# Gram matrix in two 64-column halves of the array, with a quarter of the redistribution copied by ScalarE

## The chip, the core and the metric

The kernel runs on one core of a Trainium2 chip. The metric is the device time of one execution in microseconds (us), the median of three runs. Everything is computed in 32-bit floats.

## The reference

Two identical bottleneck layers follow each other on a tensor of 64 images, 1024 channels and 14 x 14 pixels (12,544 pixels over all images). Biases, scales and shifts are inputs, and every normalisation takes its mean and variance over all images and pixels:

```python
def _conv(x, w, b, stride, pad):
    y = jax.lax.conv_general_dilated(x, w, window_strides=(stride, stride), padding=[(pad, pad), (pad, pad)], ...)
    return y + b.reshape(1, -1, 1, 1)
def _bn(x, gamma, beta):
    mean = jnp.mean(x, axis=(0, 2, 3), keepdims=True)
    var = jnp.var(x, axis=(0, 2, 3), keepdims=True)
    xn = (x - mean) * jax.lax.rsqrt(var + EPS)
    return gamma.reshape(1, -1, 1, 1) * xn + beta.reshape(1, -1, 1, 1)
# one layer; x has 1024 channels, the middle has 256
out = jax.nn.relu(_bn(_conv(x, w1, b1, 1, 0), g1, be1))      # 1x1, 1024 -> 256
out = jax.nn.relu(_bn(_conv(out, w2, b2, 1, 1), g2, be2))    # 3x3, 256 -> 256
out = _bn(_conv(out, w3, b3, 1, 0), g3, be3)                 # 1x1, 256 -> 1024
out = jax.nn.softplus(residual_scale)[0] * out
return jax.nn.relu(x + out)
```

## The kernel before

The 256 middle channels of all 12,544 pixels stay in SBUF as one tile `y_all`: 128 partitions, two channel slots `s`, 12,544 pixels. Each layer has the stages conv1 (1x1), conv2 (3x3, by a fast algorithm with few products), then a stage called the Gram stage here, then conv3 (1x1) with the residual.

The Gram stage exists because the third normalisation needs the mean and the variance of conv3's output before that output is used. Instead of computing conv3 twice, the kernel computes the 256 x 256 Gram matrix of the normalised conv2 output over all pixels (the sum over pixels of channel times channel) and the channel sums. From these and the weights `conv3_stats` (L1099) gets the mean and variance of all 1024 output channels.

For a Gram matrix the array needs pixels on the partitions, while `y_all` has channels there. So `gram` (L994) makes transposed tiles `zt`: 128 pixels on the partitions, two such blocks per tile (`CH = 2`), and 256 channels plus a column of ones along the row. There are six `zt` buffers. 12,544 pixels are 98 blocks, taken two at a time: 49 pairs.

- Normalising: `norm_to` (L1012) goes through `y_all` in pieces. ScalarE applies scale, shift and relu (L544), then VectorE subtracts a constant per channel (`less`, L1010), once for each of the two slots. The pieces have 256, 512, 1536, 832 and then six times 1568 pixels; the six are called A to F here.
- The first seven pairs (`FIRST = 7`) go by TensorE: four 128 x 128 transposes into PSUM (L1040), then one VectorE copy into `zt` (L1046).
- The other 42 pairs go by VectorE's 32 x 32 block transpose (`by_vector`, L1049). That needs the four 32-channel groups brought onto the right partitions first. `spread(k)` (L1024) does so for 1536 pixels at a time, `k = 0 .. 6`, six pairs each: sixteen transfers, from partition group `j` to partition group `i` for all `i, j`, each of 32 partitions x 2 slots x 384 pixels (96 KB). Nine are issued on SP's queue and seven on POOL's. In the four with `i == j` the data keep their partitions. The target `homes[k % 2]` is one of two buffers, so `spread(k + 2)` can only begin when the transposes of `spread(k)` have read it. The buffers are named `ws` and `home` in the first layer, `home` both in the second.
- The products: for each block of 128 pixels two matmuls, `cp` with 128 channels as the stationary operand and 257 columns moving (channels 0 to 255 and the ones), and `ap` with the other 128 channels and 129 columns. The part below the diagonal is not computed. In the trace every 32-bit matmul appears as two passes, each with a weight load of its own (x2 in the rows).

```python
matmul(g0, before[:, c, 0:P], before[:, c, :], start=first, stop=last)
matmul(g1, before[:, c, P:M], before[:, c, P:], start=first, stop=last)
```

`conv3_stats` scales the two PSUM results into SBUF (`g0` on VectorE, L1106, `g1` on ScalarE, L1107), doubles the part above the diagonal (`off`, L1108), multiplies by the weights in two halves of 512 columns with three matmuls each (L1123 to L1125), multiplies elementwise by the weights (L1128) and adds over partitions with a ones operand. A matmul group of conv3 that is needed later anyway stands in TensorE's queue between the last Gram matmul and the first of `conv3_stats`.

Order: matmuls, and instructions wrapped in `tc.keep_in_program_order` (`less`, the copies, the transposes, everything through `act`), stand in their engine's queue as written. Others are placed by a scheduler. `pairs` (L1059) is the generator that sets the order by hand: its table `then` says after which of the first seven pairs a piece is normalised or a `spread` is issued.[...]

Of the kernel before, what the change touches and what calls it, by code (L numbers as in the profile page):

```python
# [37 lines left out]
FP = mybir.dt.float32  # L38
AF = mybir.ActivationFunctionType
ALU = mybir.AluOpType  # L40

P = 128
N, C, H, W = 64, 1024, 14, 14
HW = H * W
M = 256
CS = C // P
MS = M // P
# [5 lines left out]
NPX = N * HW  # L53
CH = 2
NZT = 6

FIRST, LAST = 7, 0
RUN = 3 * P
STEP = 4 * RUN
# [7 lines left out]
GPX = GI * HW  # L67
# [20 lines left out]
def bottlenecks(ctx: ExitStack, tc: tile.TileContext, x, w1s, w2s, w3s, pars, out):  # L88
    nc = tc.nc
# [5 lines left out]
    y_all = keep.tile([P, MS, NPX], FP, tag="y", name="y")  # L95
# [70 lines left out]
    def matmul(*args, **kw):  # L166

        tc.keep_in_program_order(nc.tensor.matmul(*args, **kw))  # L168
# [160 lines left out]
    def act(*args, **kw):  # L329

        tc.keep_in_program_order(nc.scalar.activation(*args, **kw))  # L331
# [209 lines left out]
    def norm(s, y, aff, act=nc.scalar.activation):  # L541

        scale, shift = aff
        act(y, y, AF.Relu, bias=shift[:, s : s + 1], scale=scale[:, s : s + 1])  # L544
# [449 lines left out]
    def gram(psum, pool, homes, aff, minus_c, beside):  # L994

        g0, g1 = psum.tile(M + 1, "cp"), psum.tile(P + 1, "ap")
        zts = [pool.tile([P, CH, M + 1], FP, tag=f"zt{i}", name=f"zt{i}") for i in range(NZT)]
        for zt in zts:  # L1000
            nc.gpsimd.memset(zt[:, :, M:], 1.0)
        zts = itertools.cycle(zts)

        head = 3 * CH * P
        start = FIRST * CH * P
        bounds = [0, CH * P, head, head + STEP, *range(2 * GPX, NPX + 1, GPX)]
        pieces = list(zip(bounds, bounds[1:]))

        def less(s, y):
            tc.keep_in_program_order(nc.vector.tensor_scalar(y, y, minus_c[:, s : s + 1], None, ALU.add))  # L1010

        def norm_to(end):  # L1012

            while pieces and pieces[0][0] < end:
                a, e = pieces.pop(0)
                for s in reversed(range(MS)):
                    y = y_all[:, s, a:e]
                    if a == 0 and s == 1:
                        norm_vector(s, y, aff, minus_c[:, s : s + 1])
                    else:  # L1020
                        norm(s, y, aff)
                        less(s, y)

        def spread(k):  # L1024

            first = start + k * STEP if k else head
            norm_to(first + STEP)
            x = homes[k % 2][:, : MS * STEP].rearrange("p (s j f) -> p s j f", s=MS, j=4)
            for i, j in itertools.product(range(4), range(4)):
                queue = nc.gpsimd if 4 * i + j in (1, 3, 6, 8, 10, 13, 15) else nc.sync  # L1030
                a = first + i * RUN
                queue.dma_start(out=x[32 * i : 32 * i + 32, :, j], in_=y_all[32 * j : 32 * j + 32, :, a : a + RUN])
            return x.rearrange("p s j f -> p (s j) f")

        def by_tensor(a):
            tp = psum.tile(CH * M)
            for c in range(CH):
                for s in range(MS):
                    tc.keep_in_program_order(
                        nc.tensor.transpose(  # L1040
                            tp[:, (c * MS + s) * P : (c * MS + s + 1) * P],
                            y_all[:, s, a + c * P : a + (c + 1) * P], ident,
                        )
                    )
            zt = next(zts)
            tc.keep_in_program_order(nc.vector.tensor_copy(zt[:, :, :M], tp.rearrange("p (c m) -> p c m", c=CH)))  # L1046
            return zt

        def by_vector(x, i):  # L1049
            zt = next(zts)  # L1050
            tc.keep_in_program_order(
                nc.vector.transpose(
                    zt[:, :, :M].rearrange("p b (n c) -> p b n c", c=32),
                    x[:, :, i * CH * 32 : (i + 1) * CH * 32].rearrange("p n (b r) -> p b n r", r=32),
                )
            )
            return zt

        def pairs():  # L1059

            norm_to(head)
            then = {
                1: lambda: ready.append(spread(0)),
                2: partial(norm_to, 2 * GPX),
                4: partial(norm_to, 3 * GPX),
                5: lambda: ready.append(spread(1)),
            }
            for i in range(FIRST):
                a = i * CH * P
                yield by_tensor(a if a < head else a + STEP)  # L1070
                if i == 0:
                    busy(psum, "ax", 1)
                if i in then:
                    then[i]()
            for k in range(STEPS):
                x = ready.pop(0)
                for i in range(RUN // (CH * 32)):
                    yield by_vector(x, i)
                if k + 2 < STEPS:
                    ready.append(spread(k + 2))  # L1080
            norm_to(NPX)
            for i in range(LAST):
                yield by_tensor(NPX - (LAST - i) * CH * P)

        ready = []
        total = NPX // (CH * P)
        before = None
        for k, zt in enumerate(itertools.chain(pairs(), (None,))):
            if before is not None:
                for c in range(CH):  # L1090
                    first, last = k == 1 and c == 0, k == total and c == CH - 1
                    matmul(g0, before[:, c, 0:P], before[:, c, :], start=first, stop=last)
                    matmul(g1, before[:, c, P:M], before[:, c, P:], start=first, stop=last)
            before = zt
            if k in beside:
                beside[k]()
        return g0, g1

    def conv3_stats(psum, one, grams, w3, mv, tags, spare):  # L1099


        g0p, g1p = grams
        g0 = one.tile([P, M + 1], FP, tag="g0", name="g0")
        g1 = one.tile([P, P + 1], FP, tag="g1", name="g1")
        off = one.tile([P, P], FP, tag="goff", name="goff")
        nc.vector.tensor_scalar(g0, g0p, 1.0 / NPX, None, ALU.mult)  # L1106
        nc.scalar.activation(g1, g1p, AF.Copy, scale=1.0 / NPX)  # L1107
        nc.vector.tensor_scalar(off, g0[:, P:M], 2.0, None, ALU.mult)  # L1108
        means = g0[:, M:], g1[:, P:]
        wide = 64  # L1110
        sums = [psum.tile(CS * wide, tag).rearrange("p (o k) -> p o k", k=wide) for tag in ("ax", "ap")]
        ones = one.tile([P, 1], FP, tag="ones", name="ones")
        nc.vector.memset(ones, 1.0)
        ones = ones[:, :1].to_broadcast([P, wide])
        by_mean, w = spare[:, :C], [w3[:, s].rearrange("p o c -> p (o c)") for s in range(MS)]
        nc.vector.tensor_scalar(by_mean, w[0], means[0], None, ALU.mult)
        nc.vector.scalar_tensor_tensor(by_mean, w[1], means[1], by_mean, ALU.mult, ALU.add)
        half = CS // 2
        q = one.tile([P, MS, C], FP, tag="q", name="q")
        for h in range(2):  # L1120
            cols = slice(h * half, (h + 1) * half)
            t0, t1 = (psum.tile(half * P, tag) for tag in tags[2 * h : 2 * h + 2])
            matmul(t0, g0[:, 0:P], w3[:, 0, cols, :], start=True, stop=True)  # L1123
            matmul(t1, off, w3[:, 0, cols, :], start=True, stop=False)
            matmul(t1, g1[:, 0:P], w3[:, 1, cols, :], start=False, stop=True)  # L1125
            qs = [q[:, s, h * half * P : (h + 1) * half * P] for s in range(MS)]
            for s, t in ((0, t0), (1, t1)):
                nc.vector.tensor_mul(qs[s], t, w3[:, s, cols, :].rearrange("p o c -> p (o c)"))  # L1128
            nc.vector.tensor_add(qs[0], qs[0], qs[1])
        for o in range(CS):  # L1130
            matmul(sums[0][:, o], by_mean[:, o * P : (o + 1) * P], ones, start=True, stop=True)
        for o in range(CS):
            matmul(sums[1][:, o], q[:, 0, o * P : (o + 1) * P], ones, start=True, stop=True)
        nc.vector.tensor_copy(mv[:, :, 0], sums[0][:, :, 0])
        nc.vector.tensor_copy(mv[:, :, 1], sums[1][:, :, 0])
        sq = small.tile([P, CS], FP, tag="sq", name="sq")
        nc.vector.tensor_mul(sq, mv[:, :, 0], mv[:, :, 0])
        nc.vector.tensor_sub(mv[:, :, 1], mv[:, :, 1], sq)
# [193 lines left out]
    with tc.tile_pool(name="first", bufs=1) as one, tc.tile_pool(  # L1332
        name="first_x", bufs=4
# [133 lines left out]
```

## Time and profile before

| | us |
|---|---|
| median of 3 runs | 1944.43 |
| lowest and highest | 1944.18, 1944.73 |
| the profiled execution's own time | 1944.06 |
| its span in the trace | 1942.3 |
| Gram stage of layer 0: first ScalarE normalisation | 586.49 |
| first matmul of pair 7 | 602.63 |
| first matmul after the last Gram product | 659.77 |
| the same three in layer 1 | 1552.01, 1568.15, 1624.75 |

The last rows are start times within the span. From the first normalisation to the end of the Gram products it takes 73.3 us in layer 0 and 72.7 us in layer 1. "Idle before" at the end of a row is the time in which the engine had nothing to do before that row's first instruction, with what ended it. Times given as "offset" in what follows count from the first ScalarE normalisation of the layer.

### The profile page before, as it was taken

The numbers are of one execution on the slowest core, as the hardware profiler recorded it, in microseconds if no ns is written. First come the engines' busy times: TensorE is split into PE (matmuls) and PEld (weight loads), VectorE is DVE, ScalarE is ACT, GpSimd is POOL, SyncE is SP. The second block draws the span as 40 slices with busy tenths as digits, with TensorE's granted clock in tenths as the row PEclk, the third lists the DMA queues.
The fourth block names the chain that finished last, engine by engine and source line by source line (L and its number), as shares of the span: only waits on it lengthen the run. The fifth ranks groups of instructions, "written<-read, shape, count | busy, mean of one in ns | idle before, by whom it ended". The sixth has DMA issues, their size and how long they took to land.

```text
span 1942.3 us, 27081 instructions
## 1 busy us (share of the span) xinstructions
PE 1918.6 (99%) x9438; PEld 1612.1 (83%) x9438; DVE 1544.3 (80%) x2473; ACT 1046.2 (54%) x2098; POOL 575.1 (30%) x674
## 2 busy tenths in 40 slices
PE   9999999999999999999999999999999999999999
PEld 5555557999997799999999999989999987555555
DVE  5778667999998667776776767689999975888886
ACT  2222214677765055555555555456777651666666
POOL 0111100212105133433333334302121051666664
PEclk9999999999999999999999999999999999999999
DMA  7777634887948634444444444258788486899998
GB/s 291 273 250 263 235 129 157 204 221 202 230 141 207 197 137 187 175 166 166 181 185 167 166 178 180 108 181 209 215 208 225 140 194 233 279 334 335 333 342 300
DMA packets 201849, 413.91 MB, mean 213 GB/s; under 512 B 37809, under 2 KB 178001, under 8 KB 185201
## 3 DMA queue, kind: packets, MB, share of 16 engines
q1 hardware_dynamic: 161728, 324.66, 49.0%
q0 software_dynamic: 34368, 36.45, 9.3%
q10 hardware_dynamic: 5616, 51.06, 6.3%
q8 instruction: 75, 1.23, 0.3%
q14 instruction: 62, 0.50, 0.1%
HBM read 263.75 MB, written 115.34 MB: 195 GB/s over the span
## 4 chain that ended last, share of the span: by engine, by line
PE 92%; DVE 5%; DMA 1%; ACT 1%; issue 1%; SPq 0%; POOL 0%; DVEq 0%; ACTq 0%
PE cy L168 17%; PE ay L168 17%; PE columns L168 13%; PE cp L168 12%; PE ap L168 10%; PE m L168 6%; PE l L168 6%; PE cx L168 5%; PE ax L168 4%; PE ps L168 1%; DMA home<-y 1%; ACT y L544 1%; DVE v L628 0%; DVE sums L622 0%; DVE steps L697 0%
## 5 line engine op out<-in xcount | busy, mean ns | idle before, releaser
L331 ACT ACTIVATE cu<-cy,scale 128x196 f32<-128x196 f32 (+1 forms) x552 | 256.7, 474 | 277.5 <-PE cy L168 271.3
L168 PE MATMUL columns<-v,ub 128*128 128x224 f32 (+1 forms) x1536 | 300.7, 337 | 0.0
L331 ACT ACTIVATE x<-x,shift 128x392 f32<-128x392 f32 x428 | 241.1, 613 | 59.5 <-POOL x L490 53.1
L168 PEld LDWEIGHTS columns<-v,ub 128*128 128x128 f32 x1536 | 269.2, 188 | 2.8
L464 DVE SCALAR_TENSOR_TENSOR x<-cp,scale,x 128x196 f32<-128x196 f32 (+1 forms) x368 | 178.2, 484 | 97.2 <-PE cp L168 96.1
L168 PE MATMUL cy<-ct,ws 128*128 128x196 f32 (+1 forms) x736 | 221.9, 383 | 1.1 <-ACT cu L331 1.1
L485 POOL TENSOR_TENSOR x<-x,cu 128x196 f32<-128x196 f32 (+1 forms) x184 | 159.3, 866 | 172.1 <-ACT cu L331 162.5
L168 PE MATMUL ay<-at,ws 128*128 128x196 f32 (+1 forms) x752 | 209.1, 381 | 0.0
L490 POOL TENSOR_TENSOR x<-x,cu 128x392 f32<-128x392 f32 x124 | 125.9, 1016 | 192.8 <-DVE x L464 188.1
L168 PEld LDWEIGHTS ay<-at,ws 128*128 128x128 f32 x752 | 136.5, 190 | 33.4
L168 PEld LDWEIGHTS cy<-ct,ws 128*128 128x128 f32 x736 | 133.3, 190 | 36.4 <-ACT cu L331 4.2
L168 PE MATMUL l<-diffs,ub 128*128 128x224 f32 (+1 forms) x768 | 149.1, 337 | 2.6 <-PE columns L168 2.6
L511 POOL TENSOR_TENSOR x<-x,cu 128x392 f32<-128x392 f32 x120 | 121.9, 1017 | 85.9 <-DVE x L464 62.4
L168 PE MATMUL m<-sums,ua 128*128 128x224 f32 (+1 forms) x752 | 145.9, 337 | 1.5 <-DVE sums L622 1.5
L168 PEld LDWEIGHTS l<-diffs,ub 128*128 128x128 f32 x768 | 134.3, 189 | 4.4 <-PE columns L168 3.9
L331 ACT ACTIVATE au<-ay 128x196 f32<-128x196 f32 (+1 forms) x141 | 53.8, 381 | 155.2 <-PE ay L168 152.4
L464 DVE SCALAR_TENSOR_TENSOR x<-cx,scale,x 128x196 f32<-128x196 f32 (+1 forms) x184 | 89.1, 484 | 57.4 <-PE cx L168 57.4
L168 PEld LDWEIGHTS m<-sums,ua 128*128 128x128 f32 x752 | 131.3, 189 | 3.3 <-DVE sums L622 2.9
L168 PE MATMUL cx<-y,w 128*128 128x196 f32 (+1 forms) x404 | 124.1, 392 | 0.4 <-DVE x L1148 0.4
L168 PE MATMUL cy<-y,w 128*128 128x196 f32 (+1 forms) x404 | 123.8, 392 | 0.0
L168 PE MATMUL cp<-zt 128*128 128x257 f32 x392 | 118.0, 382 | 1.8 <-DVE zt L1046 1.7
L168 PE MATMUL cp<-y,ws 128*128 128x196 f32 (+1 forms) x368 | 113.6, 390 | 0.9 <-DVE x L464 0.9
(216 smaller groups left out, 3924.8 us busy)
## 6 DMA issues: line engine op xcount, KB each, us to landing
x<-in_x SPq DMA_DIRECT2D x62, 1568.0 KB, 6.8
ub<-u SPq DMA_DIRECT2D x94, 768.0 KB, 5.2
x<-mid SPq DMA_DIRECT2D x32, 1568.0 KB, 8.2
mid<-x ACTq DMA_DIRECT2D x31, 1568.0 KB, 5.1
out<-x SPq DMA_DIRECT2D x123, 392.0 KB, 5.7
ua<-u SPq DMA_DIRECT2D x94, 256.0 KB, 3.0
u<-y POOLq DMA_DIRECT2D x48, 256.0 KB, 5.8
home<-y SPq DMA_DIRECT2D x90, 96.0 KB, 4.3
```

Source lines behind the costliest of these rows:

```text
L168: tc.keep_in_program_order(nc.tensor.matmul(*args, **kw))
L331: tc.keep_in_program_order(nc.scalar.activation(*args, **kw))
L464: nc.vector.scalar_tensor_tensor(v, bank, self.scale[:, o : o + 1], v, ALU.mult, ALU.add)
L485: nc.gpsimd.tensor_add(self.part(1, 1), self.part(1, 1), u3)
L490: nc.gpsimd.tensor_add(v, v, self.u12)
L511: nc.gpsimd.tensor_add(v, v, self.u12[:, i * self.n : (i + 1) * self.n])
L544: act(y, y, AF.Relu, bias=shift[:, s : s + 1], scale=scale[:, s : s + 1])
```

## The change

There are three parts.

1. The products. The 256 channels are taken as four quarters of 64. For each block of 128 pixels there are now four matmuls with 64 stationary columns each, two in the left half of the array's columns and two in the right half (`tile_position`), with 193, 193, 129 and 130 moving columns. `zt` has a column of ones at both ends (258 wide). Each quarter is multiplied with the quarters after it, and the corner (quarter 3 with quarter 0) is taken in the last one, whose moving operand is in two pieces.
2. The statistics. The four PSUM pieces are scaled into two tiles by multiplication with constant tiles `by` (1 or 2 over the number of pixels), and the weight products take four matmuls per half instead of three.
3. The redistribution. `spread` issues only the twelve transfers with `i != j`, seven on SP and five on POOL. The new `stay(k)` makes the other four copies on ScalarE, in program order, and the normalisations go through `act` too, so that their place among the copies is fixed: `stay(0)` stands after the 832-pixel piece and ahead of A, `stay(1)` ahead of C, `stay(2)` ahead of E, `stay(3)` ahead of F, and `stay(4)` to `stay(6)` after all of them. On VectorE the `less` of D moves up, so that C and D both stand between the transposes of `spread(0)` and those of `spread(1)`.

```diff
+Q = P // 2
...
-        g0, g1 = psum.tile(M + 1, "cp"), psum.tile(P + 1, "ap")
-        zts = [pool.tile([P, CH, M + 1], FP, tag=f"zt{i}", name=f"zt{i}") for i in range(NZT)]
+        upper, lower = psum.tile(3 * Q + 1, "cp"), psum.tile(2 * Q + 2, "ap")
+        zts = [pool.tile([P, CH, M + 2], FP, tag=f"zt{i}", name=f"zt{i}") for i in range(NZT)]
         for zt in zts:
-            nc.gpsimd.memset(zt[:, :, M:], 1.0)
+            nc.gpsimd.memset(zt[:, :, 0 : M + 2 : M + 1], 1.0)
...
+        def ends(v):
+            (step, n), (_, _) = v.ap
+            return bass.AP(v.tensor, v.offset + 1, [[step, n], [3 * Q, 2], [1, Q + 1]])
...
+        by = [pool.tile([P, n], FP, tag=f"by{i}", name=f"by{i}") for i, n in enumerate((3 * Q + 1, 2 * Q + 2))]
+        gs = [pool.tile([P, M + 2], FP, tag=f"g{i}", name=f"g{i}") for i in range(MS)]
...
-                        norm(s, y, aff)
+                        norm(s, y, aff, act)
                         less(s, y)
+        def home(k):
+            return homes[k % 2][:, : MS * STEP].rearrange("p (s j f) -> p s j f", s=MS, j=4)
+        def first_of(k):
+            return start + k * STEP if k else head
+        def stay(k):
+            for i in range(4):
+                here, a = slice(32 * i, 32 * i + 32), first_of(k) + i * RUN
+                act(home(k)[here, :, i], y_all[here, :, a : a + RUN], AF.Copy)
         def spread(k):
-            first = start + k * STEP if k else head
+            first = first_of(k)
             norm_to(first + STEP)
-            x = homes[k % 2][:, : MS * STEP].rearrange("p (s j f) -> p s j f", s=MS, j=4)
-            for i, j in itertools.product(range(4), range(4)):
-                queue = nc.gpsimd if 4 * i + j in (1, 3, 6, 8, 10, 13, 15) else nc.sync
+            x = home(k)
+            for n, (i, j) in enumerate(itertools.permutations(range(4), 2)):
+                queue = nc.gpsimd if n in (1, 3, 6, 8, 10) else nc.sync
...
                 1: lambda: ready.append(spread(0)),
-                2: partial(norm_to, 2 * GPX),
+                2: lambda: (norm_to(2 * GPX), stay(0)),
                 4: partial(norm_to, 3 * GPX),
-                5: lambda: ready.append(spread(1)),
+                5: lambda: (ready.append(spread(1)), stay(1)),
...
                 if k + 2 < STEPS:
                     ready.append(spread(k + 2))
+                    norm_to(first_of(k + 2) + 2 * STEP)
+                    stay(k + 2)
...
-                    matmul(g0, before[:, c, 0:P], before[:, c, :], start=first, stop=last)
-                    matmul(g1, before[:, c, P:M], before[:, c, P:], start=first, stop=last)
+                    v = before[:, c]
+                    for q, with_ in enumerate((v[:, : 3 * Q + 1], v[:, Q + 1 :], v[:, 2 * Q + 1 :], ends(v))):
+                        here = slice(q % 2 * Q, q % 2 * Q + Q)
+                        to = (upper, lower)[q // 2][here]
+                        to = to[:, : 2 * Q + 1] if q == 2 else to
+                        if q == 3:
+                            to = to.rearrange("p (k m) -> p k m", k=2)
+                        matmul(
+                            to, v[:, 1 + q * Q : 1 + q * Q + Q], with_, start=first, stop=last,
+                            tile_position=(0, q % 2 * Q), skip_group_check=True,
+                        )
...
-        nc.vector.tensor_scalar(g0, g0p, 1.0 / NPX, None, ALU.mult)
-        nc.scalar.activation(g1, g1p, AF.Copy, scale=1.0 / NPX)
-        nc.vector.tensor_scalar(off, g0[:, P:M], 2.0, None, ALU.mult)
+        def scaled(g, a, ps, by):
+            nc.vector.tensor_mul(g[:, a : a + ps.shape[1]], ps, by[:, : ps.shape[1]])
+        scaled(g0[low], 0, upper[low], by[0][low])
+        scaled(g0[high], Q + 1, upper[high], by[0][high])
+        scaled(g1[low], 2 * Q + 1, lower[low, : 2 * Q + 1], by[1][low])
+        n = Q + 1
+        for a, k in (1, 0), (3 * Q + 1, 1):
+            scaled(g1[high], a, lower[high, k * n : k * n + n], by[1][high, k * n : k * n + n])
+        nc.scalar.activation(g0[high, 0:1], g0[high, M + 1 :], AF.Copy)
...
-            matmul(t0, g0[:, 0:P], w3[:, 0, cols, :], start=True, stop=True)
-            matmul(t1, off, w3[:, 0, cols, :], start=True, stop=False)
-            matmul(t1, g1[:, 0:P], w3[:, 1, cols, :], start=False, stop=True)
+            for i, g in enumerate((g0, g1)):
+                for n, t in enumerate((t0, t1)):
+                    matmul(t, g[:, 1 + n * P : 1 + n * P + P], w3[:, i, cols, :], start=i == 0, stop=i == 1)
```

More of the change, by code (lines that the diff above doesn't have):

```diff
@@ L994, in gram @@
     def gram(psum, pool, homes, aff, minus_c, beside):
-        g0, g1 = psum.tile(M + 1, "cp"), psum.tile(P + 1, "ap")
-        zts = [pool.tile([P, CH, M + 1], FP, tag=f"zt{i}", name=f"zt{i}") for i in range(NZT)]
+        upper, lower = psum.tile(3 * Q + 1, "cp"), psum.tile(2 * Q + 2, "ap")
+        zts = [pool.tile([P, CH, M + 2], FP, tag=f"zt{i}", name=f"zt{i}") for i in range(NZT)]
         for zt in zts:
-            nc.gpsimd.memset(zt[:, :, M:], 1.0)
+            nc.gpsimd.memset(zt[:, :, 0 : M + 2 : M + 1], 1.0)
         zts = itertools.cycle(zts)
+        def ends(v):
[3 more added lines that the diff above has]
+        gs = [pool.tile([P, M + 2], FP, tag=f"g{i}", name=f"g{i}") for i in range(MS)]
+        once, twice = 1.0 / NPX, 2.0 / NPX
+        for g in gs:
+            nc.gpsimd.memset(g, 0.0)
+        low, high = slice(0, Q), slice(Q, P)
+        for i, here, cols, value in (
+            (0, low, slice(0, Q + 1), once), (0, low, slice(Q + 1, 3 * Q + 1), twice),
+            (0, high, slice(0, Q), once), (0, high, slice(Q, 3 * Q), twice),
+            (0, high, slice(3 * Q, 3 * Q + 1), once),
+            (1, low, slice(0, Q), once), (1, low, slice(Q, 2 * Q), twice), (1, low, slice(2 * Q, 2 * Q + 1), once),
+            (1, high, slice(0, Q), twice), (1, high, slice(Q, Q + 1), 0.0), (1, high, slice(Q + 1, 2 * Q + 2), once),
+        ):
+            nc.gpsimd.memset(by[i][here, cols], value)
         head = 3 * CH * P
@@ L1045, in by_tensor @@
             zt = next(zts)
-            tc.keep_in_program_order(nc.vector.tensor_copy(zt[:, :, :M], tp.rearrange("p (c m) -> p c m", c=CH)))
+            tc.keep_in_program_order(
+                nc.vector.tensor_copy(zt[:, :, 1 : M + 1], tp.rearrange("p (c m) -> p c m", c=CH))
+            )
             return zt
@@ L1052, in by_vector @@
                 nc.vector.transpose(
-                    zt[:, :, :M].rearrange("p b (n c) -> p b n c", c=32),
+                    zt[:, :, 1 : M + 1].rearrange("p b (n c) -> p b n c", c=32),
                     x[:, :, i * CH * 32 : (i + 1) * CH * 32].rearrange("p n (b r) -> p b n r", r=32),
@@ L1091, in gram @@
                     first, last = k == 1 and c == 0, k == total and c == CH - 1
-                    matmul(g0, before[:, c, 0:P], before[:, c, :], start=first, stop=last)
-                    matmul(g1, before[:, c, P:M], before[:, c, P:], start=first, stop=last)
+                    v = before[:, c]
[8 more added lines that the diff above has]
+                            tile_position=(0, q % 2 * Q), skip_group_check=True,
+                        )
             before = zt
@@ L1096, in gram @@
                 beside[k]()
-        return g0, g1
+        return upper, lower, by, gs
     def conv3_stats(psum, one, grams, w3, mv, tags, spare):
[L1102 to L1105, printed above, removed]
-        nc.vector.tensor_scalar(g0, g0p, 1.0 / NPX, None, ALU.mult)
-        nc.scalar.activation(g1, g1p, AF.Copy, scale=1.0 / NPX)
-        nc.vector.tensor_scalar(off, g0[:, P:M], 2.0, None, ALU.mult)
-        means = g0[:, M:], g1[:, P:]
+        upper, lower, by, (g0, g1) = grams
+        low, high = slice(0, Q), slice(Q, P)
+        def scaled(g, a, ps, by):
[7 more added lines that the diff above has]
+        nc.scalar.activation(g0[high, 0:1], g0[high, M + 1 :], AF.Copy)
+        means = g0[:, 0:1], g1[:, M + 1 :]
         wide = 64
```

## The prediction

> **What bounds the kernel now.** I read the page first (its busy times, then the costliest groups), then the busy times by stretch of the Gram stage, then the timelines of TensorE, VectorE and ScalarE there.
>
> ```profile
> PE 1918.6 (99%) x9438; PEld 1612.1 (83%) x9438; DVE 1544.3 (80%) x2473; ACT 1046.2 (54%) x2098; POOL 575.1 (30%) x674
> ...
> L168 PE MATMUL cp<-zt 128*128 128x257 f32 x392 | 118.0, 382 | 1.8 <-DVE zt L1046 1.7
> ```
>
> TensorE is busy 99% of the span, so a stage is worth what its matmuls cost. The busy time by stretch, for the start, the steady part and the statistics of layer 0, and the first two of layer 1:
>
> ```profile
> 586.50:602.60 16.10, 13.39 (x81) 10.75 (x79) 13.45 (x22) 16.10 (x13) 7.00 (x10) 1.00 0.83 225
> 602.60:659.80 57.20, 57.09 (x345) 52.06 (x346) 39.20 (x60) 10.00 (x7) 23.15 (x40) 1.00 0.92 245
> 659.80:669.75 9.95, 9.95 (x50) 6.52 (x49) 6.85 (x12) 0.28 (x1) 0.00 (x0) 1.00 0.11 21
> 1552.00:1568.10 16.10, 13.40 (x81) 10.75 (x79) 13.44 (x22) 16.09 (x13) 6.98 (x10) 1.00 0.64 165
> 1568.10:1624.80 56.70, 56.65 (x345) 51.94 (x346) 36.72 (x55) 10.02 (x7) 23.06 (x40) 1.00 0.94 265
> ```
>
> Columns: stretch, length, busy TensorE, weight loads, VectorE, ScalarE, POOL, granted clock, share of the DMA engines, GB/s. At the start ScalarE is full and TensorE is not. From 602.6 on TensorE is full, and so, nearly (0.92), are the DMA engines. TensorE's timeline:
>
> ```profile
> 602.63 0.70 PE L168 MATMUL cp<-zt 128*128 128x257 f32 x2 [0.85 <-DVE zt L1046]
> 603.16 0.39 PE L168 MATMUL ap<-zt 128*128 128x129 f32 x2
> 603.39 0.60 PE L168 MATMUL cp<-zt 128*128 128x257 f32 x2
> 603.82 0.38 PE L168 MATMUL ap<-zt 128*128 128x129 f32 x2
> 604.04 0.60 PE L168 MATMUL cp<-zt 128*128 128x257 f32 x2
> ...
> 661.09 1.02 PE L168 MATMUL cy<-w,g 128*128 128x512 f32 x2
> 661.94 1.02 PE L168 MATMUL cp<-w,goff 128*128 128x512 f32 x2
> 662.80 1.02 PE L168 MATMUL cp<-w,g 128*128 128x512 f32 x2
> 663.66 1.02 PE L168 MATMUL cy<-w,g 128*128 128x512 f32 x2
> ```
>
> Start to start is what counts: a block takes 0.655 us (603.39 to 604.04), a 512-column matmul 0.86 us (661.09 to 661.94). A line through 512 columns (860 ns) and 386 columns in two matmuls (655 ns) gives 2 passes x (0.833 ns a column + about 3 ns). 43 pairs from pair 7 to the end are 86 x 0.655 = 56.4 us of the 57.14 between 602.63 and 659.77.
>
> The engines that feed it:
>
> ```profile
> 586.49 26.11 ACT L544 ACTIVATE y<-y,shift,scale 128x256 f32<-128x256 f32 x19 [1.08 <-DVE shift L1277]
> ...
> 597.51 1.98 DVE L1010 TENSOR_SCALAR y<-y,minus_c 128x1568 f32<-128x1568 f32 x2
> 600.00 1.98 DVE L1010 TENSOR_SCALAR y<-y,minus_c 128x1568 f32<-128x1568 f32 x2
> 601.88 0.69 DVE L1046 COPY zt<-ay 128x512 f32<-128x512 f32 x1
> 602.53 3.68 DVE L1052 STREAM_TRANSPOSE zt<-ws 128x512 f32<-128x512 f32 x6
> 606.13 1.94 DVE L1010 TENSOR_SCALAR y<-y,minus_c 128x1568 f32<-128x1568 f32 x2
> 611.24 3.68 DVE L1052 STREAM_TRANSPOSE zt<-home 128x512 f32<-128x512 f32 x6 [3.17 <-DMA home<-y]
> ...
> 606.24 6.48 SPq L1032 DMA_DIRECT2D ws<-y  x9
> ```
>
> ScalarE normalises without a break for 26.1 us. VectorE's queue mixes `less` with the transposes; whatever `less` waits for, the transposes behind it wait for. The transfers of one `spread` take about 10 us from first issue to last landing, and from the second spread's transposes (611.24) to the seventh's (647.33 in the same timeline) is 36.1 us, 7.2 us per spread, beside TensorE's 6 x 1.31 = 7.9.
>
> **Part 1, the products.** 64 stationary columns: passes of 193 columns take 161 + 3 = 164 ns, of 129 or 130 columns 111. Nothing in this trace shows two matmuls in two halves of the array, so the block is bounded from both sides. If both halves run freely beside each other, a half has 2 x (164 + 111) = 550 ns a block, against 655. If the halves run one after the other, 1100 ns. Weight loads: sixteen 64-column matmuls (`ax<-ones,home`, from 666.24 to the next group at 667.97) come every 108 ns, though 64 moving columns need 56, so a 128-column load takes 108 ns. If 64 columns load in half of that, eight loads take 432 ns and lie beside the 550; if not, 864 ns and they bound.
>
> Two rules of the Trainium skill bear on this. The page "TensorEngine Tiling (Array Packing)", Key Properties, says that tiles operate independently and can load and multiply in parallel: 550. The page "TensorE: Matmul & The Clock Gate", Part 3, speaks against: matmuls start and end strictly in program order. With two passes each, the second pass of a quarter holds up the first of the next, which stands in the idle half. Laid out: quarter 0 at 0 and 164 ns, quarter 1 at 164 and 328, quarter 2 at 328 and 439 (its end at 549), quarter 3 at 492 and 603, the next block's quarter 0 at 603. So 603 ns. The same section's measured 2.38 for three column tiles is 79% of three; at 79% of two a block takes an estimated 1100 / 1.59 = 693. No run here shows any of them. I take 550[...].
>
> **Part 3, the start.** This is where the gain is cut. ScalarE gets 28 copies a layer of 32 partitions x 768 elements.
>
> ```profile
> L331 ACT ACTIVATE y<-y 128x512 f32<-128x512 f32 x48 | 28.6, 625 | 57.5 <-DVE y L204 39.6 <-DVE y L201 17.6
> L331 ACT ACTIVATE y<-y 128x384 f32<-128x384 f32 x16 | 7.4, 512 | 3.8 <-DMA u<-y 3.8
> ```
>
> By these copies, 0.88 ns an element: 768 take 0.85 us, 0.79 start to start (1568-element normalisations last 1.68 and start every 1.59). Bounds: 0.63 (the 512 row) to 0.97 (the 832 normalisation); I take 0.79, 3.15 a `stay`. Its place: the 832 pieces end at offset 7.0 (593.48). Then (offsets) `stay(0)` to 10.15, A to 13.3, B to 16.5, `stay(1)` to 19.65, C to 22.8, D to 26.0. `less` needs 1.0 behind each. VectorE: `less` of A ends 14.35, copy of pair 6 at 15.0, `less` of B 17.55, copy of pair 7 at 18.2 instead of 16.0, transposes of `spread(0)` to 21.8, `less` of C 23.85, of D 27.05, first tile of `spread(1)` at 27.65. TensorE: pair 7 at 18.25, then seven pairs of 1.10 to 25.95, then it waits 1.7 for `spread(1)`. Behind that ScalarE makes a `stay` and a piece, 3.15 + 3.17 = 6.3 us, per spread, below 6.6, until F is done; later spreads need only their `stay`. End: 27.7 + 36 pairs x 1.10 = 67.3, against 73.28 and 72.74: 6.0 and 5.4 saved.
>
> The transfers: four fewer of 96 KB on the queues of a spread, two each from SP (0.70 us each by 6.48 / 9) and POOL (0.62). Bandwidth falls from 7.2 us a spread to 5.4, under 6.6. From issue to landing I take 10 x 7 / 9 = 7.8 us, upper end the old 10: spread 2, issued at 21.8, is wanted at 33.4, spread 3, issued at 30.7, at 40.3. They stay hidden by 2 us, at the old 10 with nothing to spare. Without `stay` the same products would hang on 7.2 us a spread, 3.6 us a layer lost. SP comes sooner to the loads of `x`, which then run beside the last spreads; those have some 4 us of slack. POOL's 13 new memsets (at the old row's 0.1 us or so, at most 0.3) lie before 592.98, when its first transfer is issued: hidden, 4 us at worst if not.
>
> The wider `zt` changes no count of elements in copies or transposes: nothing.
>
> **Part 2, the statistics.** One 512-column matmul more per half: 2 x 0.86 = 1.72 us a layer, in a stretch where TensorE is full (9.95 of 9.95): all of it on the path. The scaling is five VectorE multiplications instead of two plus one on ScalarE. By the PSUM row of 196 columns (0.42 us, `x<-cp,scale,x`) two of 193 end 0.8 us after the last product, all by 1.5. The first weight product comes 1.32 us after the last Gram product (659.77 to 661.09), behind the conv3 group, and needs the first two; the third comes 3.0 after it and needs all. Hidden; without the conv3 group 0.8 us a layer.
>
> **Sum.** Layer 0: -6.0 + 1.7; layer 1: -5.4 + 1.7; together -8.0. On the profiled 1944.06 that gives 1936.1, and the median stands 0.4 above it: 1936.
>
> **The rivals.**
> 1. Strict order, 603 ns a block. Seven pairs of 1.21 end at 26.7, the start hides as much; end 27.7 + 36 x 1.206 = 71.1, saved 2.2 and 1.6, less 3.4: -0.4, 1944. For it: the rule above.[...]
> 2. Slower: the halves don't overlap well enough. The place is the 86 blocks from pair 7 on. It decides from 606 ns a block: (73.0 - 1.7 - 27.7) / 36 = 1.21 us a pair. From 633 ns it is 0.2% slower. Priced at 693 ns: pair 7 at 18.25 + 43 x 1.386 = 77.9, +4.6 and +5.2, +3.4: +13, 1957. If a 64-column load costs 108 ns: 864 ns, 43 x 1.73, end 92.6: +43, 1987. If nothing overlaps: 1100 ns, end 112.9: +83, 2027. For it: 386 columns become 645, so without overlap there is no gain at all, and nothing in this trace shows an overlap.
> 3. The change gains on TensorE and hangs on ScalarE: each 0.18 us more per copy moves the start by 1.4 us a layer (8 copies lie ahead of D), 2.9 in all: 1939. It widens the first case only.
>
> **How the numbers follow.** Free overlap 0.41, strict order 0.22, partial overlap (630 to 700 ns) 0.14, loads 0.10, none 0.13. The likeliest alone: 1933 (copies at 0.63) to 1941 (copies at 0.97, transfers at 10 us), and down to 1931 for about 1 us a layer that the laid-out queues may miss. The range takes in all but the last case: 1931 to 1990. 0.2%, 3.9 us, is about what a measurement of this kernel can tell from no change. Faster by more: 0.42 (free overlap, and a little of strict order with a better start). Within: 0.19, nearly all strict order. Slower: 0.39.
>
> **What would show it.** Start to start of two blocks after 620: 0.55, 0.60 or 1.1 us. Matmul rows `cp<-zt` of both halves starting within nanoseconds of each other, or one after the other. VectorE's first transpose at offset 18.2 and TensorE idle by 1 to 2 us before `spread(1)`. The weight products of each layer's statistics show sixteen passes instead of twelve, and the stretch is 1.7 us longer. I am wrong if the block takes over 606 ns, or if VectorE waits for transfers or ScalarE after 625.

## The result, and the profile after

| | before | after |
|---|---|---|
| median | 1944.51 us (10 runs) | 1939.18 us (10 runs) |
| lowest and highest | 1943.52, 1944.73 | 1937.86, 1940.83 |
| profiled execution, own time | 1944.06 | 1940.6 |
| its span | 1942.3 | 1938.8 |

The ratio is 0.9974, with a 95% interval of 0.9966 to 0.9982: 5.3 us faster, where 8 us were predicted. Line numbers of the changed kernel are some tens higher: L168 is now L170, L1010 is L1033, L1052 is L1089. ScalarE's normalisations and copies stand at L333, the line of `act`.

The page of the changed kernel, engine totals:

```profile
PE 1906.2 (98%) x10230; PEld 1599.6 (83%) x10230; DVE 1547.2 (80%) x2479; ACT 1093.2 (56%) x2154; POOL 565.0 (29%) x672
```

TensorE has 12.4 us less to do, and the span is only 3.5 us shorter: the rest has turned into idle TensorE. (This execution is 1.4 us longer than the median; experiment 6 shows a part of why.) Where TensorE is idle is told by the busy time by stretch in layer 0 (columns as before: length, TensorE, weight loads, VectorE, ScalarE, POOL, clock, DMA share, GB/s):

```profile
586.43:605.02 18.59, 13.34 (x129) 9.27 (x127) 13.81 (x22) 18.45 (x18) 6.46 (x10) 1.00 0.63 191
605.02:614.85 9.83, 7.90 (x112) 7.21 (x113) 8.23 (x12) 9.73 (x9) 4.04 (x6) 1.00 0.71 174
614.85:655.10 40.25, 39.76 (x575) 37.76 (x576) 31.14 (x48) 21.37 (x22) 13.10 (x20) 1.00 0.76 233
```

Up to pair 7 it now takes 18.59 us instead of 16.14, with 5.2 us of TensorE idle (2.7 before); between pair 7 and the second spread 1.9 us are idle; from there TensorE is full but for 0.5 us, and the DMA engines, 0.92 before, are at 0.76. TensorE's timeline:

```profile
601.34 0.63 PE L1075 MATMUL ay<-ident,y 128*128 128x128 f32 x4 [1.38 <-DVE y L1033]
...
605.02 0.55 PE L170 MATMUL cp<-zt 128*64 128x193 f32 x4 [1.80 <-DVE zt L1082]
605.40 0.39 PE L170 MATMUL ap<-zt 128*64 128x129 f32 x4
605.62 0.50 PE L170 MATMUL cp<-zt 128*64 128x193 f32 x4
605.95 0.39 PE L170 MATMUL ap<-zt 128*64 128x129 f32 x4
606.17 0.50 PE L170 MATMUL cp<-zt 128*64 128x193 f32 x4
...
614.85 0.55 PE L170 MATMUL cp<-zt 128*64 128x193 f32 x4 [1.93 <-DVE zt L1089]
...
628.85 0.55 PE L170 MATMUL cp<-zt 128*64 128x193 f32 x4 [0.49 <-DVE zt L1089]
...
655.32 1.58 PE L170 MATMUL ay<-y,w 128*128 128x392 f32 x4
656.74 1.02 PE L170 MATMUL cy<-w,g 128*128 128x512 f32 x2
657.60 1.02 PE L170 MATMUL cp<-w,g 128*128 128x512 f32 x2
```

The first row is the four transposes of pair 7. From 605.62 to 606.17 a block takes 0.55 us, as laid out for halves that run freely. The products end at 655.32, offset 68.89 (73.28 before); in layer 1 at offset 69.73 (72.74 before). That the two halves really run at once is seen when the timeline is asked for in narrow slices. The slice up to 625.50 holds two passes of `cp` that have just begun, and the slice from 625.80 the other two, begun at 625.62: four passes of 164 ns, two and two.

```profile
625.45 0.33 PE L170 MATMUL cp<-zt 128*64 128x193 f32 x2
...
625.62 0.33 PE L170 MATMUL cp<-zt 128*64 128x193 f32 x2
```

ScalarE and VectorE at the start, from their timelines:

```profile
586.43 7.08 ACT L333 ACTIVATE y<-y,shift,scale 128x256 f32<-128x256 f32 x7 [1.07 <-DVE shift L1331]
593.41 3.42 ACT L333 ACTIVATE ws<-y 32x768 f32<-32x768 f32 x4
596.85 6.45 ACT L333 ACTIVATE y<-y,shift,scale 128x1568 f32<-128x1568 f32 x4
603.21 3.42 ACT L333 ACTIVATE home<-y 32x768 f32<-32x768 f32 x4
606.65 6.45 ACT L333 ACTIVATE y<-y,shift,scale 128x1568 f32<-128x1568 f32 x4
613.01 3.42 ACT L333 ACTIVATE ws<-y 32x768 f32<-32x768 f32 x4
616.46 3.28 ACT L333 ACTIVATE y<-y,shift,scale 128x1568 f32<-128x1568 f32 x2
619.64 3.42 ACT L333 ACTIVATE home<-y 32x768 f32<-32x768 f32 x4
...
603.33 1.03 DVE L1033 TENSOR_SCALAR y<-y,minus_c 128x1568 f32<-128x1568 f32 x1 [0.53 <-ACT y L333]
604.29 0.68 DVE L1082 COPY zt<-ay 128x512 f32<-128x512 f32 x1
604.89 3.66 DVE L1089 STREAM_TRANSPOSE zt<-ws 128x512 f32<-128x512 f32 x6
...
613.14 1.04 DVE L1033 TENSOR_SCALAR y<-y,minus_c 128x1568 f32<-128x1568 f32 x1 [0.55 <-ACT y L333]
614.09 3.67 DVE L1089 STREAM_TRANSPOSE zt<-home 128x512 f32<-128x512 f32 x6
...
633.10 3.68 DVE L1089 STREAM_TRANSPOSE zt<-ws 128x512 f32<-128x512 f32 x6 [1.34 <-ACT home L333]
639.12 3.86 DVE L1089 STREAM_TRANSPOSE zt<-home 128x512 f32<-128x512 f32 x6 [2.34 <-DMA home<-y]
644.77 2.59 DVE L1089 STREAM_TRANSPOSE zt<-ws 128x512 f32<-128x512 f32 x4 [1.80 <-DMA ws<-y]
```

The chain is the one of the prediction: four copies on ScalarE (593.41), then A and B, then `less` of B on VectorE (603.33), and only behind it the copy of pair 7 (604.29), which TensorE waits for. VectorE worked in the order of its queue here: the transposes of pair 7 were over by 602.0, and VectorE had nothing to do for 0.53 us before 603.33, but the copy still stood behind `less`. Then four more copies, C and D, `less` of D (613.14), and behind it the transposes of the second spread. Four copies take 3.44 us start to start (593.41 to 596.85), 0.86 each.

### The profile page after: what moved, and what is told of

Its sections match the earlier page's. It is cut to its first block, busy times and chain, and to the rows that moved or that the text cites. A ratio compares the mean times of both kernels' runs of the same rounds, so it can differ in the third digit from the quotient of the medians.

```text
span 1938.8 us, 28681 instructions
## 1 busy us (share of the span) xinstructions
PE 1906.2 (98%) x10230; PEld 1599.6 (83%) x10230; DVE 1547.2 (80%) x2479; ACT 1093.2 (56%) x2154; POOL 565.0 (29%) x672
## 5 line engine op out<-in xcount | busy, mean ns | idle before, releaser
L333 ACT ACTIVATE cu<-cy,scale 128x196 f32<-128x196 f32 (+1 forms) x552 | 256.9, 474 | 277.8 <-PE cy L170 272.5
L170 PE MATMUL columns<-v,ub 128*128 128x224 f32 (+1 forms) x1536 | 300.7, 337 | 0.0
L333 ACT ACTIVATE x<-x,shift 128x392 f32<-128x392 f32 x428 | 241.0, 613 | 59.6 <-POOL x L492 52.9
L170 PEld LDWEIGHTS columns<-v,ub 128*128 128x128 f32 x1536 | 269.3, 188 | 2.8
L170 PE MATMUL cy<-ct,ws 128*128 128x196 f32 (+1 forms) x736 | 221.9, 383 | 1.1 <-ACT cu L333 1.1
L170 PE MATMUL ay<-at,ws 128*128 128x196 f32 (+1 forms) x752 | 209.1, 381 | 0.0
L170 PEld LDWEIGHTS ay<-at,ws 128*128 128x128 f32 x752 | 136.5, 190 | 33.4
L170 PEld LDWEIGHTS cy<-ct,ws 128*128 128x128 f32 x736 | 133.3, 190 | 36.4 <-ACT cu L333 4.4
L170 PE MATMUL l<-diffs,ub 128*128 128x224 f32 (+1 forms) x768 | 149.2, 337 | 2.6 <-PE columns L170 2.6
L170 PE MATMUL m<-sums,ua 128*128 128x224 f32 (+1 forms) x752 | 145.9, 337 | 1.1 <-DVE sums L624 1.1
L333 ACT ACTIVATE au<-ay 128x196 f32<-128x196 f32 (+1 forms) x141 | 53.8, 381 | 156.7 <-PE ay L170 153.9
L170 PEld LDWEIGHTS l<-diffs,ub 128*128 128x128 f32 x768 | 134.3, 189 | 4.5 <-PE columns L170 3.9
L170 PEld LDWEIGHTS m<-sums,ua 128*128 128x128 f32 x752 | 131.3, 189 | 2.9 <-DVE sums L624 2.5
L170 PE MATMUL cx<-y,w 128*128 128x196 f32 (+1 forms) x404 | 124.2, 393 | 0.4 <-DVE x L1202 0.4
L170 PE MATMUL cy<-y,w 128*128 128x196 f32 (+1 forms) x404 | 123.8, 392 | 0.0
L170 PE MATMUL cp<-y,ws 128*128 128x196 f32 (+1 forms) x368 | 113.6, 390 | 1.5 <-DVE x L466 1.4
L760 ACT ACTIVATE columns<-m 128x448 f32<-128x448 f32 (+1 forms) x160 | 78.4, 490 | 59.8 <-PE m L170 57.3
```

What stands on the lines that cost most here:

```text
L760: nc.scalar.activation(v, m, AF.Copy)
```

## The experiments

**1. The products alone.** Everything of parts 1 and 2, with the old sixteen transfers and the old order.

```diff
-            for n, (i, j) in enumerate(itertools.permutations(range(4), 2)):
-                queue = nc.gpsimd if n in (1, 3, 6, 8, 10) else nc.sync
+            for i, j in itertools.product(range(4), range(4)):
+                queue = nc.gpsimd if 4 * i + j in (1, 3, 6, 8, 10, 13, 15) else nc.sync
...
-                2: lambda: (norm_to(2 * GPX), stay(0)),
+                2: partial(norm_to, 2 * GPX),
-                5: lambda: (ready.append(spread(1)), stay(1)),
+                5: lambda: ready.append(spread(1)),
...
-                    norm_to(first_of(k + 2) + 2 * STEP)
-                    stay(k + 2)
```

> Only the new products and statistics; all sixteen transfers of every spread and the order of the normalisations as before. Theory (the halves overlap freely at 550 ns a block, the start and the feeding decide the rest): pair 7 starts at offset 16.1 again, the block stays 550 ns, and the spreads land as before, the seventh at offset 60 to 61, so the products end near 68 in both layers, about 5 us sooner than before; with 3.4 us more in the statistics some 1937 us, no worse than the whole change at 1939. Rival (the transfers would have been the bound, and the ScalarE copies are what makes the change pay): the products end past 70, 1942 us or more.

Measured: 1939.7 us (1938.44 to 1940.69), ratio 0.9976 (0.9966 to 0.9985). Pair 7 starts at offset 16.3 and the products end at 68.8 and 67.4, as expected; the profiled run was 1938.44, near the sum, the median 1.3 higher. So the products alone are worth the whole change: the copies take back at the start what they give later. VectorE's timeline shows what the copies relieve, since here it waits for transfers before nearly every spread:

```profile
610.86 3.68 DVE L1089 STREAM_TRANSPOSE zt<-home 128x512 f32<-128x512 f32 x6 [2.58 <-DMA home<-y]
618.77 3.68 DVE L1089 STREAM_TRANSPOSE zt<-ws 128x512 f32<-128x512 f32 x6 [2.37 <-DMA home<-y]
...
647.55 3.68 DVE L1089 STREAM_TRANSPOSE zt<-ws 128x512 f32<-128x512 f32 x6 [4.50 <-DMA ws<-y]
```

From the second spread to the seventh: 36.7 us, 7.3 per spread, while TensorE needs 6.6.

**2. The copies alone**, with the old products: part 3 of the diff put into the kernel before.

> Only the ScalarE copies and the new order, with the old products of 257 and 129 columns. Theory: the start costs the same as in the whole change, pair 7 near offset 18.6, first tile of the second spread near 28.4, and from there 36 pairs of 1.31 us: end near 75.6, 2 to 3 us later per layer, 1949 to 1950 us. Rival (the copies relieve the transfers and cost nothing on the path): 1944 us, the same as before.

Measured: 1949.09 us (1948.73 to 1949.49), ratio 1.0025 (1.0015 to 1.0034): slower by 4.7 us. TensorE's timeline:

```profile
605.43 0.70 PE L168 MATMUL cp<-zt 128*128 128x257 f32 x2 [1.53 <-DVE zt L1058]
...
615.26 0.70 PE L168 MATMUL cp<-zt 128*128 128x257 f32 x2 [0.36 <-DVE zt L1064]
```

Pair 7 at offset 18.59 (605.43 - 586.84), the second spread at 28.42, the same as in the whole change; in layer 1 the products end at 75.8 (72.7 before). The start's cost belongs to the copies and their order, not to the products.

**3. The order of the quarters.** This is the test of the strict order.

```diff
-for q, with_ in enumerate((v[:, : 3 * Q + 1], v[:, Q + 1 :], v[:, 2 * Q + 1 :], ends(v))):
+for q, with_ in ((0, v[:, : 3 * Q + 1]), (2, v[:, 2 * Q + 1 :]), (1, v[:, Q + 1 :]), (3, ends(v))):
```

> The whole change with the four quarters issued in the order 0, 2, 1, 3: the two of the left half first, then the two of the right. Theory (each half of the array has its own queue): the block stays at 550 ns and the time at 1939 us. Rival (matmuls start strictly in the order of the program, and the alternation of the halves hid it): the left half of the next block waits for the right half of this one, 880 ns a block by the same lay-out, about 65 us more.

Measured: 1939.63 us in one run. TensorE's timeline (the rows gather passes by the tile they write, so they look as before; in the queue `ap` now comes ahead of the second `cp`):

```profile
624.98 0.55 PE L170 MATMUL cp<-zt 128*64 128x193 f32 x4
625.31 0.44 PE L170 MATMUL ap<-zt 128*64 128x129 f32 x4
625.53 0.55 PE L170 MATMUL cp<-zt 128*64 128x193 f32 x4
```

0.55 us a block. Asked for in narrower slices, the four `cp` passes of this block start at 624.98, 625.04, 625.15 and 625.21, and its first `ap` pass only at 625.31. So the second `cp` starts beside the first, 0.06 us behind it, although the `ap` in front of it in the queue has to wait for its half. Matmuls for one half don't hold up matmuls for the other, at least over these few. The rival is out.

**4. The start undone.** The whole change, but the first spread by sixteen transfers, so without `stay(0)`, and no early normalising: the copies of each later spread stand behind the piece that it needs.

```diff
-            for n, (i, j) in enumerate(itertools.permutations(range(4), 2)):
-                queue = nc.gpsimd if n in (1, 3, 6, 8, 10) else nc.sync
+            if k:
+                moves = [(i, j, n in (1, 3, 6, 8, 10)) for n, (i, j) in enumerate(itertools.permutations(range(4), 2))]
+            else:
+                moves = [(i, j, 4 * i + j in (1, 3, 6, 8, 10, 13, 15)) for i in range(4) for j in range(4)]
+            for i, j, pool_queue in moves:
+                queue = nc.gpsimd if pool_queue else nc.sync
...
-                2: lambda: (norm_to(2 * GPX), stay(0)),
+                2: partial(norm_to, 2 * GPX),
...
-                    norm_to(first_of(k + 2) + 2 * STEP)
                     stay(k + 2)
```

> The whole change, except that the first spread keeps its sixteen transfers, stay(1) to stay(6) follow behind the piece that their spread needs, and no piece is normalised early. Theory (the copies ahead of pieces A to D are what the start costs, and the idle TensorE there is what lowers its clock afterwards): pair 7 at offset 16.1, no gap before the second spread, granted clock 1.00 throughout, products end near offset 64 in both layers, 1929 to 1931 us. Rival (the later spreads wait for transfers that take 10 us from issue to landing, whatever the start): VectorE waits for transfers before the third to fifth spreads, and the time stays above 1934.

Measured: 1930.34 us (1929.47 to 1932.23), ratio 0.9930 (0.9916 to 0.9944): 14 us below the kernel before and nearly 9 below the change. By stretch, layer 0, up to pair 7 and from pair 7 to the end of the products:

```profile
586.56:602.84 16.28, 13.27 (x130) 9.23 (x128) 13.41 (x21) 16.21 (x15) 7.03 (x11) 1.00 0.83 225
602.84:650.15 47.31, 47.31 (x689) 46.34 (x689) 39.00 (x60) 30.10 (x29) 17.41 (x27) 1.00 0.80 234
```

TensorE has no idle time from pair 7 on: 43 pairs of 1.10. The products end at offsets 63.6 and 64.0. VectorE does wait a little for the later spreads' transfers (seven on SP instead of nine), before the third spread and, for 0.43 us, before the fifth:

```profile
615.05 3.67 DVE L1093 STREAM_TRANSPOSE zt<-ws 128x512 f32<-128x512 f32 x6 [0.54 <-DMA ws<-y]
```

TensorE has tiles left each time, and the time is far below 1934: the rival is out. Of the time between the two versions' ends in layer 0 (68.9 against 63.6), 2.3 us are the later pair 7 and the rest the waits behind it.

**5. Which half of the start.** As 4, its other edits with it, but with the early normalising kept.

```diff
...
-                2: lambda: (norm_to(2 * GPX), stay(0)),
+                2: partial(norm_to, 2 * GPX),
```

> The whole change with the first spread by sixteen transfers again and without stay(0), but with the early normalising of the piece after next kept (C and D both before the transposes of the second spread). It parts the start's cost between stay(0) and the moved pieces. Theory (in-order queues): pair 7 at offset 16.3, as in the version with both taken away; D ends on ScalarE near offset 23.2, so the first tile of the second spread comes near 25.0 and TensorE waits about 1 us there; 1932 to 1934 us. Rival (all of the cost was stay(0)): 1930 us and no wait before the second spread.

Measured: 1933.0 us (1932.85 to 1933.82), ratio 0.9943 (0.9929 to 0.9956). TensorE's timeline:

```profile
602.71 0.55 PE L170 MATMUL cp<-zt 128*64 128x193 f32 x4 [0.91 <-DVE zt L1086]
...
611.45 0.55 PE L170 MATMUL cp<-zt 128*64 128x193 f32 x4 [0.85 <-DVE zt L1093]
...
625.39 0.55 PE L170 MATMUL cp<-zt 128*64 128x193 f32 x4 [0.56 <-DVE zt L1093]
```

Pair 7 at offset 16.28 (602.71 - 586.43), 0.85 us of idle before the second spread at 25.02: both as expected. Of the 8.8 us between the change and version 4, `stay(0)` and its place make 6.2, the moved normalising 2.7.

**6. The gaps filled.** In the profile of layer 1 the granted clock was not 1.00 everywhere. By stretches of 4 us behind the two gaps:

```profile
1574.00:1578.00 4.00, 2.08 (x32) 1.71 (x28) 3.16 (x4) 3.95 (x5) 1.44 (x2) 1.00 0.86 226
1578.00:1582.00 4.00, 4.00 (x40) 3.57 (x38) 3.53 (x6) 3.95 (x4) 0.85 (x1) 0.62 0.05 12
1582.00:1586.00 4.00, 4.00 (x58) 3.75 (x56) 3.49 (x6) 3.90 (x6) 2.72 (x5) 0.95 0.88 225
```

After a stretch with TensorE half idle the clock is at 0.62 and 0.95, 1.7 us of full clock lost: (1 - 0.62) x 4 + (1 - 0.95) x 4. In slices of 1 us the clock is 0.50 in each from 1579 to 1582, and the blocks there start 1.07 us apart (1579.58 and 1580.65) instead of 0.55. Layer 0 of the same execution has the same two gaps and stays at 1.00. The experiment puts matmuls without use into the two gaps:

```diff
             before = zt
+            if k in (FIRST - 1, FIRST - 1 + RUN // (CH * 32)):
+                busy(psum, "ax", 2)
```

> The whole change with two idle-filling matmuls of 448 columns (0.75 us each) before the products of pair 7 and two before the first pair of the second spread, in the two gaps of 1.8 and 1.9 us; their results are not used. Theory (those gaps make the clock gate halve TensorE's clock for some 3.4 us in a part of the executions, at 1.7 us each time): granted clock 1.000 in every run, the runs between 1937.8 and 1939.4 us, none at 1940 or more. Rival (the dips come by chance, or from something else than the gaps): clocks of 0.998 and 0.999 appear again in about 3 runs of 10, and the runs spread over 3 us as before.

> The whole change, unaltered, beside the others on the same chip: 1938 to 1941 us, with the granted clock at 0.998 or 0.999 in a part of the runs, and those runs some 1.8 us longer than the others.

Measured: with the gaps filled 1939.38 us (1938.54 to 1939.99), ratio 0.9974 (0.9964 to 0.9984); the change again, beside it, 1939.14 us (1938.3 to 1940.63), ratio 0.9973 (0.9963 to 0.9983). The same stretches with the gaps filled:

```profile
1574.00:1578.00 4.00, 3.94 (x34) 2.27 (x32) 3.45 (x5) 3.93 (x5) 1.09 (x2) 1.00 0.77 202
1578.00:1582.00 4.00, 4.00 (x62) 3.75 (x60) 3.20 (x5) 3.97 (x3) 1.19 (x2) 1.00 0.12 29
1582.00:1586.00 4.00, 4.00 (x62) 3.80 (x60) 3.82 (x6) 3.90 (x6) 2.38 (x4) 1.00 0.85 230
```

The clock is 1.000 in all nine runs, and layer 1's products end at offset 68.24 instead of 69.73. In the change's 18 runs the mean clock was 0.998 or 0.999 in seven, with a median of 1940.2 us, and 1.000 in eleven, with 1938.8: 1.4 apart, where 1.8 were expected. The second profile of the change (mean clock 0.998) shows the dip in both layers, at the same place:

```profile
614.00:618.00 4.00, 3.31 (x34) 2.92 (x36) 3.60 (x7) 3.92 (x5) 0.10 (x1) 0.73 0.18 41
618.00:622.00 4.00, 4.00 (x52) 3.68 (x50) 3.42 (x5) 3.95 (x4) 3.81 (x5) 0.84 0.65 168
...
1578.00:1582.00 4.00, 3.88 (x32) 3.35 (x34) 3.57 (x7) 3.95 (x4) 0.32 (x1) 0.57 0.06 12
```

Layer 0's products end at 69.7 there, against 68.9 in the first profile.

The expectation on the clock held, that on the times did not quite: no run reached 1940, but the median is not below the change's, and 0.6 above its runs at full clock. The highest runs are gone, the median is not improved. Seven in 18 against none in nine leaves some room for chance. A mean below 1.000 also doesn't tell where the clock was low: versions without this pair of gaps (numbered here by experiment) have it too (the kernel before in 4 of 35 runs, version 1 in 4 of 9, version 2 in 1 of 9, version 4 in 1 of 5, version 5 in 1 of 4), and in the profile of version 1 (0.999) the only stretch below 1.00 is the last 4.7 us, at 0.76, with 0.07 us of TensorE work in it. That the two gaps bring the dips behind them is therefore likely, and not shown beyond doubt; filling them won no time that these runs can tell.

## Why the prediction was right, and where it was too good

- **The block.** Predicted 550 ns, measured 550. Free overlap was given 0.41, strict order 0.22, and experiment 3 parts the two. Of the two rules of the Trainium skill that were weighed, "TensorEngine Tiling (Array Packing)", Key Properties (tiles operate independently), is what these traces agree with; the strict order of "TensorE: Matmul & The Clock Gate", Part 3, they don't show for the starts of matmuls in two column halves. The choice between the two (0.41 against 0.22) was a judgement with no run behind it, and that it fell on the right side is in part luck. The halves' weight loads (132 to 137 ns from start to end by the trace, 186 to 193 for 128 columns) lie beside the products.
- **The start.** The mechanism was right: `stay(0)` in front of A, VectorE's queue behind `less`. The duration of a copy was right (0.85 us predicted, 0.84 measured), but the overlap of 0.06 to 0.09 us between neighbours, taken from the normalisations, isn't there: the copies start 0.86 us apart, not 0.79. Over the eight copies ahead of D that is 0.6 us; pair 7 came at 18.59 instead of 18.25 and the second spread at 28.42 instead of 27.65. For the same reason a `stay` and a piece take ScalarE 6.63 us (613.01 to 619.64), not the 6.3 of the prediction. That is all of TensorE's 6.6 for six pairs: up to the fourth spread ScalarE sets the pace as much as TensorE does, and in layer 1 the transposes of these spreads start 6.63 and 6.64 us apart (1576.83, 1583.46, 1590.10).
- **After the second spread.** 27.65 + 36 x 1.10 should have ended at 67.3. Layer 0 ended at 68.9: 0.8 from the start, 0.5 before the fourth spread (628.85; there VectorE is idle for 0.43 us, and the profile names no releaser, so the cause stays open; a small instruction for the next layer, `minus_c`, runs just ahead of it, and in layer 1, where none stands there, VectorE goes straight on), the rest small. Layer 1 ended at 69.7, and at 68.2 with the gaps filled: about 1.5 us of it is the clock, a cost that stood nowhere in the sum.
- **The transfers.** Issue to landing of one fell from 4.3 to 3.4 us in the median, about the 7 / 9 assumed. From the first issue of a spread to the transposes that wait for it 7.3 us (631.78 to 639.12) and 8.0 us (636.80 to 644.77) go by in layer 0, for 7.8 predicted. One of the prediction's own signs of being wrong did appear: after 625 VectorE waits for transfers or ScalarE (1.34, 2.34 and 1.80 us, in the rows above). The sign was set too tight: TensorE still had tiles to work on and has no wait behind 628.85.
- **The statistics.** From the first matmul after the products to the first after the sums: 659.77 to 669.75 before, 655.32 to 667.12 after, 1.82 us more for 1.72 predicted. The difference is the group after the last product, 1.42 instead of 1.32 us: its first pass takes 0.43 us to the next start, the other three 0.33. The sum had nothing for the step from 64-column to 128-column matmuls.
- **The sum.** On the profiled execution: -8.0 predicted, -3.5 measured. The missing 4.5: 1.6 and 2.4 at the two ends of the products, 0.2 in the statistics, some 0.3 spread over the rest. The eleven runs at full clock stand at 1938.8, 2.7 above the 1936.1 predicted, and that is the start (twice 0.8) and what followed it. (Two slips in the working change nothing: 86 x 0.655 is 56.3, not 56.4, and 6.48 / 9 is 0.72, not 0.70.)

The rival that ScalarE would hang was priced at 1.4 us a layer for 0.18 us more per copy; that is where part of the missing gain was, with 0.07. The other two rivals did not come about: the block takes 550 ns.

## What to carry to other kernels

Where a matmul's output is a symmetric matrix, smaller stationary blocks in two halves of the array save the part that needn't be computed, if the columns of the two halves balance and the two can run at once: here 386 moving columns became 322 and 323, one number for each half. When an engine of slack takes over work, ask what stands behind it in that engine's queue at that moment: ScalarE was 54% busy on the average and full in the first 26 us, where the copies were put. Without the first spread's copies, and with the others behind the pieces that other engines wait for, the kernel was 9 us faster. When the stage that bounds is made faster, lay out the start of its pipeline anew: here the start cost more than the whole change had gained.

## What the runs showed of the hardware

- Two 64-column matmuls in 32-bit floats, each with two passes, run side by side at the full rate of each (550 ns a block for passes that add up to 1100), and the order in which the two halves' matmuls stand in the queue made no difference (1939.63 us in one run, against 1939.18).
- A copy of 32 partitions x 768 elements on ScalarE lasts 0.84 us, and they start every 0.86 us, without the overlap of 0.09 us that the normalisations show (1.68 us long, started every 1.59). 32 partitions instead of 128 make it no shorter than the line through the 128-partition copies says (0.85 us).
- In both profiles of the change whose mean clock is below 1.000, TensorE runs at half clock for some 3.4 us (0.50 in slices of 1 us, blocks 1.07 us apart) shortly after two gaps of 1.8 and 1.9 us that lie ten us apart; in one layer of the four the same gaps had no such effect, and with the gaps filled nine runs showed no mean below 1.000. The Trainium skill's page "TensorE: Matmul & The Clock Gate", Part 1, gives half rate after an idle window of about 3.4 us; the gaps here were each shorter than that.
- Where 64-column products and 128-column transposes take turns, in the first seven pairs, a round takes 1.83 us (596.23 to 598.06), against 1.75 before (596.26 to 598.01), although its two blocks by themselves are 0.2 us shorter; the transposes alone take 0.59 us to the next start instead of 0.44. TensorE has slack there, so this cost nothing here. No run parts what takes the time.
